# Output projection of a slot-attention and feed-forward kernel: from float32 products to three float32r products on 12-bit parts, added to the residual stream in DRAM

## The chip, the cores and the metric

One core of a Trainium2 chip. The metric is the device time of one launch in microseconds (us); the engines that matter are TensorE (PE in the profile, with its weight loads PEld), VectorE (DVE), ScalarE (ACT), GpSimd (POOL) and SyncE (SP, which only issues DMAs here).

## The reference, cut to what matters

Four samples (b = 0 to 3) of 512 tokens by 512 features. Each goes through an attention block with 16 heads and then a feed-forward block, both behind a layer norm and both added to the residual stream.

```
x = x + attention(layernorm(x))
x = x + ffn(layernorm(x))

attention(x):
  q, k, s = x @ Wq, x @ Wk, clip(x @ Ws, -32, 32)       # per head 64 wide
  v, g    = x @ Wv, x @ Wg                               # per head 128 wide
  o  = softmax(causal (q k^T) over slots weighted by exp(s)) applied to v in the same causal way
  o  = o * rsqrt(mean(o^2) + eps) * g_norm_weight
  o  = o * g * sigmoid(g)
  return o @ Wo                                          # 2048 -> 512
ffn(x): silu(x @ fp8(gate) * gs) * (x @ fp8(up) * us) @ fp8(down) * ds
```

The output projection `o @ Wo` and the gate `g = x @ Wg` are what the change touches. All inputs are float32.

## The kernel before, in words

**Units.** The attention works on units: a unit is a pair of heads (g = 0 to 7, HG = 2 heads) of one sample b. They run in the order of two halves: all eight g for samples 0 and 1 in turn ((0,0), (0,1), (1,0), ... (7,1)), then all eight g for samples 2 and 3. That makes 32 units. In units with an even g the values of two head pairs are projected at once (four `project_v`); units with an odd g have no value projection and are shorter. The feed-forward block of all four samples follows, in 12 chunks of 128 hidden features per sample.

**Precision by parts.** A projection such as q, k, s, g or v does not run in float32. Activation and weight are each kept as a rounded high part, a remainder and a mixed third matrix, all float32r; `Projection.main` (L463) accumulates two products per 128-row chunk into one PSUM bank, `Projection.mixed` (L475) a third product into another, ScalarE scales the first bank out (L473), and VectorE subtracts the second (L483). `project_v` (L504) does the same for v. The weights are split once, in the first half, by pieces of 512 columns in `load_matrix` (L222: one ScalarE and two VectorE operations a piece), written to DRAM, and read back already split in the second half. The small attention products (`states`, `diagonal_blocks`, `slot_scores`, `read_out`) and the transposes are plain float32.

**The output projection.** `turn_output` (L746) transposes the scaled head output into PSUM and VectorE multiplies it by the norm weight and by the gate `sg` into `oT` (L751). `project_output(n)` (L756) multiplies, for each of four blocks n of 128 tokens, `oT` with `w_o` in float32, one matmul per head (L760), and VectorE adds the PSUM bank to the residual tile `x1[b]` in SBUF (L768). All four samples' residual streams stay in SBUF for the whole kernel. A unit's own output is projected during the next unit (`before` in `attention`).

**Order.** The order of the work is written out by hand in `attention` (L773): every engine runs its instructions in exactly this order. Side work (splitting weights in the first half; in the second half rounding the feed-forward weights to fp8 in `quantize`, L401, six VectorE operations a piece) lies in a list, and `other()` takes the next step of it at fixed places. PSUM has a pool of three banks with the tag `proj` (all projections), three single banks for transposes and small products, and two accumulators.

The tail of a unit in this order, before the change:

```
X.slot_scores(); X.value_states()
X.gate_main(0); X.softmax(); X.gate_mixed(0); X.gate_silu(0); output(...)
X.gate_main(1); X.slot_weights(); X.softmax_sum(); X.gate_mixed(1); X.gate_silu(1); exp_and_log()
output(...); X.weight_slot(); output(3); X.read_out()
```

`slot_scores` (L629) makes the scores (`ps_ok`), VectorE scales them (`okT`, L652); `softmax` (L654) transposes them (`ps_okn`), VectorE takes the maximum (L659) and subtracts it (L661), ScalarE exponentiates (L664); `slot_weights` (L676) transposes back (`ps_w`) and VectorE scales (`wT`, L681); `weight_slot` (L683) makes the masked blocks `b` (L542); `read_out` (L686) the head output (`ps_ov`), whose squares ScalarE takes (L714) for the norm; the `pow` of the norm runs on GpSimd (L719). `gate_silu` switches ScalarE's function table and `exp_and_log` switches it back.

Of the kernel before, what the change touches and what calls it, by code (L numbers as in the profile page):

```python
# [49 lines left out]
def kernel(  # L50
# [37 lines left out]
    resid = ctx.enter_context(tc.tile_pool(name="resid", bufs=1))  # L88
# [48 lines left out]
    dsc = const.tile([P, D], F32, tag="dsc", name="dsc")  # L137
# [6 lines left out]
    def load_scales():  # L144
        nc.gpsimd.dma_start(dsc, down_scale.partition_broadcast(P))
        nc.gpsimd.dma_start(srow[0:NFC, :], gate_scale.rearrange("(c p) -> c p", p=P))
        nc.gpsimd.dma_start(srow[NFC : 2 * NFC, :], up_scale.rearrange("(c p) -> c p", p=P))
        nc.gpsimd.dma_start(srow[2 * NFC : NS, :], g_norm.rearrange("(c p) -> c p", p=P))
# [12 lines left out]
    MATRICES = {"s": (Ws, HM), "k": (Wk, HM), "q": (Wq, HM), "v": (Wv, 2 * HV), "g": (Wg, HV)}  # L161
    wt = {}
    split = {}
    wo = {}
# [17 lines left out]
    for g in range(NG):  # L182
        names = [nm for nm in MATRICES if nm != "v" or g % 2 == 1]
        if g == 0:
            names = "v"
        for nm in names:
            n = g if nm != "v" else 0 if g == 0 else (g + 1) // 2
            if nm != "v" or n < NG // 2:
                parts = max(1, KC * MATRICES[nm][1] // RAW)
                to_fetch += [(nm, n, part, KC // parts) for part in range(parts)]  # L190
    fetched = [0]

    def fetch():
        if to_fetch:
            nm, g, part, chunks = to_fetch.pop(0)
            src, width = MATRICES[nm]
            tag = f"raw{fetched[0] % 2}"
            fetched[0] += 1
            w = one.tile([P, RAW], F32, tag=tag, name=f"raw_{nm}_{g}_{part}")[:, : chunks * width]
            rows = src[part * chunks * P : (part + 1) * chunks * P, g * width : (g + 1) * width]  # L200
            nc.sync.dma_start(
                w.rearrange("p (c n) -> p c n", c=chunks), rows.rearrange("(c p) n -> p c n", p=P)
            )
            raw.setdefault((nm, g), []).append(w)

    def fetch_first():

        for tag, names in (("og", "sk"), ("oT", "q"), ("sg", "g")):
            w = one.tile([P, 2, RAW // 2], F32, tag=tag, name=f"raw_{names}")
            for i, nm in enumerate(names):  # L210
                src, width = MATRICES[nm]
                to = w[:, i, :] if nm != "g" else w.rearrange("p i n -> p (i n)")
                nc.sync.dma_start(
                    to.rearrange("p (c n) -> p c n", c=KC),
                    src[:, :width].rearrange("(c p) n -> p c n", p=P),
                )
                raw[nm, 0] = [to]
            if names == "q":
                fetch()
                fetch()  # L220

    def load_matrix(nm, g, first):  # L222
        width = MATRICES[nm][1]
        w = one.tile([P, 3, KC * width], F32R, tag=f"w_{nm}", name=f"w_{nm}_{g}")
# [5 lines left out]
        pieces = KC * width // 512  # L230
# [9 lines left out]
        def rest(n):  # L240
            cols = slice(n * 512, (n + 1) * 512)
            hi, lo = w[:, 0, cols].bitcast(F32), w[:, 1, cols].bitcast(F32)
            if scale == 1.0:
                nc.vector.tensor_tensor(w[:, 1, cols], source(n), hi, ALU.subtract)
            else:
                nc.vector.scalar_tensor_tensor(
                    w[:, 1, cols], source(n), scale, hi, ALU.mult, ALU.subtract
                )
            nc.vector.scalar_tensor_tensor(w[:, 2, cols], hi, DELTA, lo, ALU.mult, ALU.subtract)
            if (n + 1) * 512 % RAW == 0 or n + 1 == pieces:  # L250
                if g > 0 or nm == "v":
                    fetch()
            if n + 1 == pieces:
                split[nm, g] = dram.tile(
                    [P, 3, KC * width], F32, tag=f"split_{nm}_{g}", name=f"split_{nm}_{g}"
                )
                nc.sync.dma_start(split[nm, g], w.bitcast(F32))
# [10 lines left out]
    def load_wo(g):  # L268
        wo[g] = one.tile([P, HG, D], F32, tag="w_o", name=f"w_o_{g}")
        nc.sync.dma_start(wo[g], Wo[g * HV : (g + 1) * HV, :].rearrange("(c p) n -> p c n", p=P))  # L270

# [9 lines left out]
    x1 = [resid.tile([P, NT, D], F32, tag=f"x1_{b}", name=f"x1_{b}") for b in range(B)]  # L281
# [104 lines left out]
    staged = []  # L386

    def stage():
        if to_round:
            c, m = to_round.pop(0)  # L390
            cols = slice(c * P, (c + 1) * P)
            tag = "qw" if (3 * c + m) % 2 else "raw0"
            w = one.tile([P, D], F32, tag=tag, name=f"qw_{c}_{m}")
            if m < 2:
                src = (gate_w, up_w)[m][:, cols].rearrange("(c p) n -> p c n", p=P)
                nc.sync.dma_start(w.rearrange("p (c n) -> p c n", n=P), src)
            else:
                nc.sync.dma_start(w, down_w[cols, :])
            staged.append((c, m, w))
# [169 lines left out]
    class Heads:  # L569


        def __init__(self, g, b):
            self.u, self.g, self.b = f"{g}_{b}", g, b
            self.v0 = g % 2 * HV

# [158 lines left out]
        def gate_main(self, h):  # L734
            if h == 0:
                self.sg = one.tile([P, HG, T], F32, tag="sg", name=f"sg_{self.u}")
            self.pg = Projection("g", self.b, h * DV, f"g_{self.u}_{h}")
            self.pg.main(self.sg[:, h, :])
# [4 lines left out]
        def gate_silu(self, h):  # L743
            nc.scalar.activation(self.sg[:, h, :], self.sg[:, h, :], AF.Silu)

        def turn_output(self, h, n_bank=None):  # L746

            if h == 0:
                self.oT = one.tile([P, HG, T], F32, tag="oT", name=f"oT_{self.u}")
            pt = transpose_4(self.og[:, h], f"ps_oT_{self.u}_{h}", n_bank)  # L750
            nc.vector.scalar_tensor_tensor(  # L751
                self.oT[:, h, :], pt.rearrange("p n t -> p (n t)"), gw, self.sg[:, h, :],
                ALU.mult, ALU.mult,
            )

        def project_output(self, n):  # L756

            pp = ps3.tile([P, D], F32, tag="proj", name=f"ps_o_{self.u}_{n}")
            for h in range(HG):
                nc.tensor.matmul(  # L760
                    pp,
                    self.oT[:, h, n * P : (n + 1) * P],
                    wo[self.g][:, h, :],
                    start=(h == 0),
                    stop=(h == HG - 1),
                )
            to = x1[self.b][:, n, :]
            nc.vector.tensor_tensor(to, to, pp, ALU.add)  # L768
# [4 lines left out]
    def attention(g, b, before, load):  # L773
# [5 lines left out]
        def output(n):  # L779
            if before:  # L780
                before.project_output(n)

# [20 lines left out]
        X.queries(None)  # L803
        load("q")
        X.turn_e()
        if even:
# [10 lines left out]
            if before:  # L817
                before.turn_output(1)
            X.query_key()
            X.values(2)  # L820
            other()
            next_step()
            X.values(3)
            load("v")
            if b > 1:
                other(1)
        else:
            if before:
                before.turn_output(0)
            X.turn_k()  # L830
            if before:
                before.turn_output(1)
            X.key_states()
            X.inverse()
            X.query_key()
            output(0)
            other()
            next_step()
            output(1)
        other()  # L840
        X.slot_scores()
        next_step()
        X.value_states()
        other()
        next_step()
        need("g")
        X.gate_main(0)
        X.softmax()
        X.gate_mixed(0)
        other()  # L850
        X.gate_silu(0)
        output(0 if even else 2)
        if before:
            next_step()
        X.gate_main(1)
        X.slot_weights()
        X.softmax_sum()
        X.gate_mixed(1)
        load("g")
        X.gate_silu(1)  # L860
        exp_and_log()
        if even:
            output(1)
            other()
            output(2)
        X.weight_slot()
        output(3)
# [23 lines left out]
    def ffn_hidden(b, c):  # L891
# [12 lines left out]
        tag = ("sg", "og", "oT")[at] if at >= 0 else ("raw0", "raw1")[c % 2]  # L904
# [6 lines left out]
    def ffn_down(b, chunks, sums):  # L911
# [37 lines left out]
    with tc.manual_schedule(engines=EVERY):  # L949
        blocks = x[0].rearrange("(n p) d -> p n d", p=P)  # L950
        for n in range(NT):
# [3 lines left out]
        load_wo(0)  # L955
        layernorm(0, 1)
        for nm in "vgskq":
            load_matrix(nm, 0, True)
        for b in range(1, B):
            nc.sync.dma_start(x1[b], x[b].rearrange("(n p) d -> p n d", p=P))  # L960
# [5 lines left out]
        for i, (g, b) in enumerate(units):  # L966
            last = i + 1 == len(units)

            def load(nm):
# [5 lines left out]
                elif nm == "o":  # L975
                    if b % 2 == 0 and i > 0:
                        load_wo(g)
# [3 lines left out]

            if i == 0 or (g, b) == (0, 2):
# [19 lines left out]
            if i == 0:  # L1002
                scale_columns()
        while work:
# [10 lines left out]
        for b in range(B):  # L1015
            need(f"xs_{b}")
            for c in range(NFC):
# [3 lines left out]
                if b == 0 and 0 < c < 3:  # L1021
                    before.turn_output(c - 1, 2)
                if b == 0 and 2 < c < 3 + NT:
                    before.project_output(c - 3)
                if c == 1 and b + 1 < B:
                    layernorm(b + 1, 2, 2)()
                if prev is not None:
# [8 lines left out]
                    else:  # L1036
                        ffn_down(pb, [(pc, parts)], sums)
# [3 lines left out]
        ffn_down(B - 1, kept + [(c, h)], sums)  # L1041
# [43 lines left out]
```

## Time and profile before

| | |
|---|---|
| median of 3 runs | 1526.57 us (1526.57 to 1530.5) |
| the profiled execution | 1527.82 us |
| its span in the trace | 1526.1 us |
| granted TensorE clock, mean | 0.996 |
| GpSimd busy | 78.5 us, 77 instructions |
| DMA moved | 149.51 MB, mean 98 GB/s |
| first score product of a split unit / first feed-forward product | 61.2 us / 1242.2 us |
| a unit with even g, second half (786.21 to 829.27 us) | 43.06 us |
| a unit with odd g, second half (721.63 to 753.92 us) | 32.29 us |

How to read the profile's lines: a group of instructions is given as line, engine, operation, output<-inputs by the program's names, shapes and count; then busy time and mean duration of one in ns; then the engine's idle time just before them and what ended it. In a timeline each row is a start, a duration, and the same description. A float32 matmul of 128x512 leaves two records, a float32r one leaves one; durations of matmuls overlap (the next starts before the end of the last), so the distance from one group's start to the next group's start is what a group costs TensorE.

### The profile page before, as it was taken

How to read it: one execution, taken by the hardware profiler on the slowest of the kernel's cores; microseconds unless marked ns; L12 is line 12 of the kernel's file. 1: busy time of each engine (PE TensorE's matmuls, PEld its weight loads, DVE VectorE, ACT ScalarE, POOL GpSimd, SP SyncE). 2: the span in 40 equal slices, each digit the busy share in tenths (PEclk: the TensorE clock that was granted, in tenths of full speed). 3: DMA queues.
4: the chain of work that ended last, by engine and by line, in shares of the span. 5: the costliest groups of instructions: out<-in, count | busy, mean ns of one | idle time of the engine just before them, and what ended most of it. 6: DMA issues, size and time to landing. Idle time of an engine off the chain costs nothing.

```text
span 1526.1 us, 21595 instructions
## 1 busy us (share of the span) xinstructions
PE 1495.5 (98%) x8821; PEld 1131.9 (74%) x8821; DVE 1014.9 (66%) x1814; ACT 558.2 (37%) x942; POOL 78.5 (5%) x77
## 2 busy tenths in 40 slices
PE   7899999999999999999999999999999999999998
PEld 4677777777777777777777777777777777888886
DVE  7677747774777477676877787778777754535333
ACT  4534333433443343442433243333333332222321
POOL 1000000000000000000000000000000000000000
PEclk9999999999999999999999999999999999999999
DMA  8133303330333052115232522243234220000000
GB/s 330 63 111 152 138 15 111 152 138 14 111 152 139 15 207 77 49 42 207 68 120 84 199 81 106 104 179 100 87 116 153 77 104 1 28 0 28 1 28 28
DMA packets 59842, 149.51 MB, mean 98 GB/s; under 512 B 3848, under 2 KB 32544, under 8 KB 56672
## 3 DMA queue, kind: packets, MB, share of 16 engines
q1 hardware_dynamic: 59280, 147.34, 26.5%
q8 instruction: 69, 1.13, 0.3%
q10 hardware_dynamic: 288, 0.52, 0.1%
q0 software_dynamic: 176, 0.28, 0.1%
q14 instruction: 29, 0.24, 0.0%
HBM read 90.45 MB, written 57.67 MB: 97 GB/s over the span
## 4 chain that ended last, share of the span: by engine, by line
PE 91%; DVE 5%; ACT 3%; issue 1%; DMA 0%; POOL 0%; ACTq 0%; DVEq 0%; POOLq 0%
PE ps_o L760 15%; PE ps_v L511 8%; PE ps_g L468 8%; PE ps_fu L880 5%; PE ps_fg L880 5%; PE ps_ov L704 4%; PE ps_v_m L511 4%; PE ps_g_m L479 4%; PE ps_s L468 3%; PE ps_k L468 3%; PE ps_q L468 3%; PE ps_fd L924 2%; PE ps_a L538 2%; PE ps_fe L924 2%; PE ps_b L538 2%; PE ps_ok L644 2%
## 5 line engine op out<-in xcount | busy, mean ns | idle before, releaser
L760 PE MATMUL ps_o<-w_o,oT 128*128 128x512 f32 x512 | 242.0, 604 | 0.0
L760 PEld LDWEIGHTS ps_o<-w_o,oT 128*128 128x128 f32 x512 | 93.2, 189 | 85.6 <-issue 75.5
L468 PE MATMUL ps_g<-xs,w_g 128*128 128x512 f32 x512 | 144.4, 423 | 0.3
L511 PE MATMUL ps_v<-w_v,xs 128*128 128x512 f32 x512 | 132.9, 401 | 0.0
L768 DVE TENSOR_TENSOR x<-x,ps_o 128x512 f32<-128x512 f32 x128 | 87.7, 685 | 56.9 <-PE ps_o L760 56.8
L468 PEld LDWEIGHTS ps_g<-xs,w_g 128*128 128x128 f32 x512 | 93.3, 188 | 36.5 <-issue 18.2
L473 ACT ACTIVATE sg<-ps_g 128x512 f32<-128x512 f32 x64 | 38.2, 597 | 214.0 <-PE ps_g L468 213.1
L719 POOL TENSOR_TENSOR rs<-rs,mhalf 128x8 f32<-128x8 f32 x32 | 56.0, 1750 | 1095.1 <-DVE rs L716 920.3
L901 DVE SCALAR_TENSOR_TENSOR h<-ps_fu,scol,act 128x512 f32<-128x512 f32 x48 | 36.0, 750 | 113.8 <-PE ps_fu L880 111.2
L511 PEld LDWEIGHTS ps_v<-w_v,xs 128*128 128x128 f32 x512 | 92.3, 188 | 20.3
L520 DVE TENSOR_TENSOR v<-v,ps_v_m 128x512 f32<-128x512 f32 x64 | 44.0, 688 | 94.5 <-PE ps_v_m L511 94.5
L519 ACT ACTIVATE v<-ps_v 128x512 f32<-128x512 f32 x64 | 38.4, 600 | 163.6 <-PE ps_v L511 163.6
L880 PE MATMUL ps_fg<-xs,wf 128*128 128x512 f32 x384 | 96.5, 393 | 0.0
L880 PE MATMUL ps_fu<-xs,wf 128*128 128x512 f32 x384 | 95.1, 390 | 1.1 <-ACT act L898 1.1
L880 PEld LDWEIGHTS ps_fu<-xs,wf 128*128 128x128 f32 x384 | 72.0, 188 | 16.7 <-ACT act L898 1.5
L880 PEld LDWEIGHTS ps_fg<-xs,wf 128*128 128x128 f32 x384 | 71.1, 188 | 14.5
L714 ACT ACTIVATE og<-ps_ov 128x512 f32<-128x512 f32 x64 | 38.2, 598 | 118.4 <-PE ps_ov L704 118.4
L715 DVE TENSOR_REDUCE rs<-og 128x4 f32<-128x512 f32 x64 | 43.9, 686 | 54.8 <-ACT og L714 54.8
L479 PE MATMUL ps_g_m<-xs,w_g 128*128 128x512 f32 x256 | 75.3, 416 | 0.0
L704 PE MATMUL ps_ov<-v,b 128*128 128x128 f32 x512 | 67.3, 286 | 3.0 <-DVE b L542 3.0
L511 PE MATMUL ps_v_m<-w_v,xs 128*128 128x512 f32 x256 | 68.8, 391 | 0.0
L468 PE MATMUL ps_s<-xs,w_s 128*128 128x512 f32 x248 | 65.8, 407 | 2.4 <-ACT xs L343 2.4
(149 smaller groups left out, 2759.2 us busy)
## 6 DMA issues: line engine op xcount, KB each, us to landing
split_v<-w_v SPq DMA_DIRECT2D x4, 3072.0 KB, 10.9
split_g<-w_g SPq DMA_DIRECT2D x8, 1536.0 KB, 6.1
w_v<-split_v SPq DMA_DIRECT2D x4, 3072.0 KB, 10.7
w_g<-split_g SPq DMA_DIRECT2D x8, 1536.0 KB, 6.7
rounded<-qw SPq DMA_DIRECT2D x36, 256.0 KB, 2.0
wf<-rounded SPq DMA_DIRECT2D x12, 768.0 KB, 5.9
w_o<-in_L_attn_Wo_dram SPq DMA_DIRECT2D x16, 512.0 KB, 3.6
split_s<-w_s SPq DMA_DIRECT2D x8, 768.0 KB, 4.2
```

The source lines that it names most:

```text
L468: nc.tensor.matmul(self.p, products(self.nm, c, self.col0, i), xs[self.b][i][:, c, :], start=(i == 0 and c == 0), stop=(i == 1 and c == KC ...
L479: nc.tensor.matmul(self.m, products(self.nm, c, self.col0, 2), xs[self.b][2][:, c, :], start=(c == 0), stop=(c == KC - 1),)
L511: nc.tensor.matmul(dst, xs[b][i][:, c, n * P : (n + 1) * P], wt["v"][:, i, c * 2 * HV : (c + 1) * 2 * HV], start=(i == which[0] and c == 0 ...
L520: nc.vector.tensor_tensor(to, to, m, ALU.subtract)
L538: nc.tensor.matmul(pa[h][:, n, :], lT[rows, cols], rT[rows, cols], start=True, stop=True)
L704: nc.tensor.matmul(po[h][:, n, :], self.bb[h][:, n, :], both_v[self.b][:, n, self.v0 + h * DV : self.v0 + (h + 1) * DV], start=False, stop ...
L715: nc.vector.tensor_reduce(rs[:, h, :], self.og[:, h], AX.X, ALU.add)
L719: nc.gpsimd.tensor_tensor(rs, rs, mhalf.rearrange("p (h n) -> p h n", h=HG), ALU.pow)
L760: nc.tensor.matmul(pp, self.oT[:, h, n * P : (n + 1) * P], wo[self.g][:, h, :], start=(h == 0), stop=(h == HG - 1),)
L768: nc.vector.tensor_tensor(to, to, pp, ALU.add)
L880: nc.tensor.matmul(pp, w[:, c * P : (c + 1) * P], xs[b][k][:, c, :], start=(c == 0 and k == 0), stop=(c == KC - 1 and k == 1),)
L924: nc.tensor.matmul(sums[n], parts[k][:, n * P : (n + 1) * P], fw[c][2], start=(c == 0 and k == 0), stop=(c == NFC - 1 and k == 1),)
```

## The change

- `Wo` becomes a sixth matrix of `MATRICES`, split by `load_matrix` like the others (two pieces of 512 columns for each g, written to DRAM in the first half and read back in the second, 1.5 MB instead of 0.5 MB).
- `turn_output` now writes gate times output into `sg` in place; `high_output` and `split_output` make the three parts of `oT` from it: per head two ScalarE and two VectorE operations more.
- `project_output(n)` does six float32r matmuls into two `proj` banks (four into `p`, two into `m`) instead of two float32 ones into one; ScalarE scales `p` into an SBUF tile `y` (two buffers).
- `add_output(n)` (new) subtracts `m` from `y` on VectorE, and a GpSimd DMA with `accum_op=add` adds `y` to `stream[b]`, a copy of the sample's residual stream in DRAM (filled by DMA from `x`). The four resident tiles are gone: `load_tokens` reads a sample's stream into one of two `x1` buffers when a layer norm needs it.
- In `attention` both gate halves and their silu move ahead of `slot_scores`; all four `output(n)` now stand between `softmax` and `read_out`, in even and odd units alike. Places of `other()` move too: one now lies behind the q projection, and in even units one lies behind `value_states`.

```diff
-    MATRICES = {"s": (Ws, HM), "k": (Wk, HM), "q": (Wq, HM), "v": (Wv, 2 * HV), "g": (Wg, HV)}
+    MATRICES = {"s": (Ws, HM), "k": (Wk, HM), "q": (Wq, HM), "g": (Wg, HV), "v": (Wv, 2 * HV), "o": (Wo, D)}
+    CHUNKS = {nm: HG if nm == "o" else KC for nm in MATRICES}
...
-    x1 = [resid.tile([P, NT, D], F32, tag=f"x1_{b}", name=f"x1_{b}") for b in range(B)]
+    stream = [dram.tile([T, D], F32, tag=f"stream_{b}", name=f"stream_{b}") for b in range(B)]
+    x1 = {}
+    def load_tokens(b, source):
+        x1[b] = two.tile([P, NT, D], F32, tag="x1", name=f"x1_{b}")
+        nc.sync.dma_start(x1[b], source[b].rearrange("(n p) d -> p n d", p=P))
...
             nc.vector.scalar_tensor_tensor(
-                self.oT[:, h, :], pt.rearrange("p n t -> p (n t)"), gw, self.sg[:, h, :],
+                self.sg[h], pt.rearrange("p n t -> p (n t)"), gw, self.sg[h],
                 ALU.mult, ALU.mult,
             )
+        def high_output(self, h):
+            nc.scalar.mul(self.oT[:, 0, h, :], self.sg[h], UNDER)
+        def split_output(self, h):
+            hi, lo, less = (self.oT[:, i, h, :] for i in range(3))
+            nc.vector.tensor_tensor(lo, self.sg[h], hi.bitcast(F32), ALU.subtract)
+            nc.vector.scalar_tensor_tensor(
+                less, lo.bitcast(F32), -1.0 / DELTA, hi.bitcast(F32), ALU.mult, ALU.add
+            )
+            nc.scalar.mul(lo, lo.bitcast(F32), 1.0 / DELTA)
         def project_output(self, n):
-            pp = ps3.tile([P, D], F32, tag="proj", name=f"ps_o_{self.u}_{n}")
-            for h in range(HG):
-                nc.tensor.matmul(pp, self.oT[:, h, n * P : (n + 1) * P], wo[self.g][:, h, :], ...)
-            to = x1[self.b][:, n, :]
-            nc.vector.tensor_tensor(to, to, pp, ALU.add)
+            p = ps3.tile([P, D], F32, tag="proj", name=name)
+            m = ps3.tile([P, D], F32, tag="proj", name=name + "_m")
+            for dst, which in ((p, (0, 1)), (m, (2,))):
+                for i in which:
+                    for h in range(HG):
+                        nc.tensor.matmul(dst, self.oT[:, i, h, n * P : (n + 1) * P],
+                            wt["o"][:, i, h * D : (h + 1) * D], ...)
+            y = two.tile([P, D], F32, tag="y", name=f"y_{self.u}_{n}")
+            nc.scalar.mul(y, p, 1.0 + DELTA)
+            self.y[n] = y, m
+        def add_output(self, n):
+            y, m = self.y.pop(n)
+            nc.vector.tensor_tensor(y, y, m, ALU.subtract)
+            nc.gpsimd.dma_start(stream[self.b][n * P : (n + 1) * P, :], y, accum_op=ALU.add)
```

The new order in `attention`, from the key states on, for a unit with odd g (even units have the same tail; their parts of `oT` are made between the value projections):

```diff
+            before.high_output(0)
+            before.high_output(1)
+            X.query_key()
+            before.split_output(0)
+            before.split_output(1)
             X.inverse()
...
+        X.gate_main(0); X.gate_mixed(0); X.gate_main(1); X.gate_mixed(1)
+        X.gate_silu(0); X.gate_silu(1); exp_and_log()
         X.slot_scores()
         X.value_states()
+        if even: other()
         X.softmax()
+        output(0)
+        before.project_output(1)
         X.slot_weights()
+        before.add_output(1)
         X.softmax_sum()
+        output(2)
         X.weight_slot()
         other()
+        output(3)
         X.read_out()
```

## The prediction, before the changed kernel had run

> **What bounds the kernel now.** I read the page's busy shares and the chain that ended last, then the PE timeline of one unit, then the DVE and ACT timelines of the same unit, and last the list of DMA issues.
>
> ```profile
> PE 1495.5 (98%) x8821; PEld 1131.9 (74%) x8821; DVE 1014.9 (66%) x1814; ACT 558.2 (37%) x942; POOL 78.5 (5%) x77
> ...
> PE 91%; DVE 5%; ACT 3%; issue 1%; DMA 0%; POOL 0%; ACTq 0%; DVEq 0%; POOLq 0%
> ```
>
> TensorE is the bound, and by the chain it waits for almost nobody. VectorE has a third of the span free, but not evenly: in the second half it is busy 25.70 us of an odd unit's 32.29. The PE timeline of that odd unit (start, duration):
>
> ```profile
> 724.45 1.98 PE L468 MATMUL ps_k<-xs,w_k 128*128 128x512 f32 x8
> 726.26 1.07 PE L479 MATMUL ps_k_m<-xs,w_k 128*128 128x512 f32 x4
> 727.17 1.98 PE L468 MATMUL ps_q<-xs,w_q 128*128 128x512 f32 x8
> ...
> 733.75 3.70 PE L760 MATMUL ps_o<-w_o,oT 128*128 128x512 f32 x8
> 737.38 0.87 PE L637 MATMUL ps_ok<-qT,sk 64*64 64x128 f32 x12
> 738.18 1.09 PE L644 MATMUL ps_ok<-a,e 128*64 128x128 f32 x16
> 739.11 0.82 PE L552 MATMUL ps_sv<-v,e 128*64 128x128 f32 x12
> 739.86 2.13 PE L468 MATMUL ps_g<-xs,w_g 128*128 128x512 f32 x8
> 741.83 0.60 PE L528 MATMUL ps_okn<-ident,okT 128*128 128x128 f32 x4
> ...
> 743.21 1.88 PE L760 MATMUL ps_o<-w_o,oT 128*128 128x512 f32 x4
> 744.52 2.42 PE L468 MATMUL ps_g<-xs,w_g 128*128 128x512 f32 x8
> 746.77 0.60 PE L528 MATMUL ps_w<-ident,ok 128*128 128x128 f32 x4
> ```
>
> Every group starts where the last one's stream ends: TensorE is never short of work, because gate products and output blocks lie between the links of the softmax chain. Costs follow from start to start. Twelve float32r products of k take 727.17 - 724.45 = 2.72 us, 0.227 each. Two float32 output blocks take 737.38 - 733.75 = 3.63, 1.82 a block.
>
> **TensorE's gain.** A block becomes six float32r products: 6 x 0.227 = 1.36. Going from float32 to float32r and back costs extra: g's first eight products, after `ps_sv`, take 1.97 where k's take 1.81, and a mixed group ahead of float32 1.02 instead of 0.91; call it 0.15 in, 0.10 out. The four output blocks stand in three runs, so 4 x 1.36 + 3 x 0.25 = 6.19, against 3.63 + 1.31 + 1.91 = 6.85 now (the last block 749.33 to 751.24). The gate, now in one run, falls from 1.97 + 1.02 + 2.25 + 1.11 = 6.35 to 5.70. Gain 1.3 in an odd unit; the same sum in an even one gives 1.4. I take **1.35 a unit, 43 us in 32 units**.
>
> **What the new order uncovers.** The gate no longer stands between the scores and their transpose.
>
> ```profile
> 739.39 0.69 DVE L652 TENSOR_TENSOR okT<-ps_ok,rzT 128x512 f32<-128x512 f32 x1 [0.15 <-PE ps_ok L644]
> ...
> 742.47 0.69 DVE L659 TENSOR_REDUCE mx<-ps_okn 128x8 f32<-128x512 f32 x1 [0.21 <-PE ps_okn L528]
> 743.19 0.69 DVE L661 TENSOR_TENSOR ok<-ps_okn,mx 128x512 f32<-128x512 f32 x1
> ```
> ```profile
> 743.92 0.63 ACT L664 ACTIVATE ok<-ok 128x512 f32<-128x512 f32 x1 [1.29 <-DVE ok L661]
> ```
>
> (A) Put the new order on these times. `okT` ends at 740.08, while `ps_sv` ends at 739.86: `ps_okn` waits 0.27 to 740.13. VectorE has the sums of `sv` until 740.94 (its rows L563 and L565), then maximum and subtraction to 742.36, ScalarE the exponential to 743.03, and behind it on ScalarE's queue stands the scaling of the first block's `p` (0.60, as L473) to 743.65. TensorE does `ps_okn` to 740.49, block 0 to 742.0, block 1's `p` to 742.9, and then block 1's `m`: of three `proj` banks it gets the one that block 0's `p` held, so it waits for that scaling until 743.7, 0.8 us. Queued behind `m` is `ps_w`, and so the rest of the unit. A costs 1.07 a unit.
>
> (B) Odd units only. ScalarE's second halves of the two `lo` parts stand ahead of gate 0's scaling-out, and gate 1's mixed product needs that bank. From the end of the `ps_a` products (733.75): hand-over 0.2, two masks 1.3, four VectorE split operations at 0.66 = 2.6, `lo` 0.6, gate 0 0.6: 739.1. TensorE gets there at 733.75 + 1.97 + 0.91 + 1.81 = 738.4. B costs 0.75. In even units the splits lie between value projections, with 0.4 to spare by the same sum: nothing; if that cover were gone, 0.6.
>
> (C) Side work moves into the chain. Second half, even units: two rounding operations (L424, L425: 1.3) between `sv` and the maximum, lengthening A: 7 x 1.3. Odd units: L412 and L413 (0.7) ahead of the q subtraction, which leaves about 0.35 late: 7 x 0.35. First half: a weight piece on ScalarE (0.6) between exponential and scaling in some five odd units: 3. Together 15.
>
> (D) The added DMAs. Nothing like an accumulating DMA is in this trace. `y` has two buffers, so ScalarE's scaling of block 2 waits until block 0's DMA has landed; block 3's `m` waits for the bank which that scaling frees, and on VectorE the masks of `b` stand behind block 2's subtraction. Count from the end of block 0's scaling: subtraction 0.69, then L (hand-over to GpSimd and landing), scaling 0.6 and two hand-overs of 0.05: `m` can start at 1.39 + L. TensorE meanwhile does `m` 0.55, `ps_w` 0.36, block 2's 1.6, `ps_b` 1.1 and block 3's `p` 1.06, arriving at 4.7. **The wait is L - 3.3 in each of 31 units.** Next by size:
>
> ```profile
> raw_sk<-in_L_attn_Ws_dram SPq DMA_DIRECT2D x1, 256.0 KB, 5.1
> ...
> dsc<-in_L_ffn_down_scale_dram POOLq DMA_DIRECT2D x1, 256.0 KB, 6.1
> ```
>
> Upper end: GpSimd's one 256 KB DMA took 6.1, but in the start-up traffic, when SP's loads of that size took 5.1 too (3.1 later: `raw_s`); plus 0.17 hand-over, L = 6.3. Lower end: the Trainium skill, "DMA: Bandwidth & Descriptors", section "Anatomy of one DMA — SWDGE (gpsimd) path", gives a GpSimd DMA 2.0 us plus its bytes at 436 GB/s: 2.6, an estimate from that page, so L = 2.8 and no wait at all. By the rule D costs 0, by the row 31 x 3.0 = 93. Value: a 256 KB store by SP takes 2.0 (`rounded`), GpSimd's path about 0.8 more (6.1 against 5.1 to 5.5), reading the destination first 1.1 more (a load's 3.1 against a store's 2.0), hand-over 0.17, and 0.35 for weight loads beside it (`w_o` triples): L = 4.4, nearer the row when its start-up share is taken off. D costs 31 x 1.1 = 34. A second rule speaks against the change: "SBUF — State Buffer", section "Who interferes with whom", says that VectorE operations in its two-port mode keep GpSimd from writing descriptors. No row here shows it; the candidates are the 0.42 us rounding operations, so it can add some tenths in the second half, inside my upper end.
>
> GpSimd's `pow` (1.67) queues behind block 3's DMA issue (0.76 for `dsc`), yet VectorE uses its result 0.9 us after it ends today: hidden, at worst 0.7 a unit. The other additions are hidden too: VectorE's block subtractions replace the additions one for one (685 ns each), ScalarE's 8 x 0.6 us a unit meet an engine busy 12.4 of 32.3 us, except where A and B name them.
>
> (E) Edges. Splitting the first `w_o` adds four VectorE operations (2.8) at the start, where VectorE is busy 38 of 50 us. In the feed-forward part the stream loads for samples 2 and 3 wait on the SP queue for the stores of an earlier sample, and VectorE's queue holds their statistics ahead of the hidden products: about 2 each. The last unit's projection there: about 1. Together 8; from 0 to 15.
>
> **The sum.** Odd: 16 x (-1.35 + 1.07 + 0.75) = +7.5. Even: 15 x (-1.35 + 1.07) = -4.2. C +15, D +34, E +8: +60. On the profiled execution's 1527.8 (span 1526.1 and 1.7 around it) 1588; the median was 1.2 lower: **1586**.
>
> **Rivals.** (1) *L below 3.3.* D vanishes, A to C and E stay: 1526.6 + 26 = 1553. For it: the rule above; against it: 6.1 in the trace. (2) *Faster: TensorE stays the bound.* One place decides, block 1's `m`: if block 0's scaling is done when TensorE arrives, so that A (0.8) goes and every later anchor of D moves 0.8 forward with L under 2.5, odd units gain 0.3 and even ones 1.1, and with TensorE filling the rest of the gaps the whole 43 less E is gained, 1526.6 - 35 = 1492. The tipping point is waits of 1.35 a unit. For it: L760 and the projections show no idle time today, and ScalarE is 37% busy. Against: the chain, whose links are all measured, is longer than the 3.5 us of work left beside it. (3) *The accumulating DMA is as slow as at start-up*, 6.3: 1526.6 + 26 + 93 = 1645.
>
> **Numbers.** The likeliest case, L from 3.3 to 5.5, 1553 to 1620: 0.55. Rival 1, 1532 to 1553: 0.15. Rival 2, 1480 to 1522: 0.15. Rival 3 and beyond, over 1620: 0.10. Gain and waits cancelling, within 0.3% (about what a measurement of this kernel can tell from no change): 0.05. So faster 0.15, same 0.05, slower 0.80. The range 1512 to 1645 leaves out most of rival 2 and the tail of rival 3.
>
> **What would show it.** Right: block products at 0.227 us each and no `ps_o` group over 1.6; TensorE idle before `ps_okn` (0.3) and before the second `ps_o` m-group (0.8) released by ScalarE; in odd units idle before gate 1's mixed product; ScalarE's third `y` released by a GpSimd DMA, with L - 3.3 of TensorE idle before the fourth m-group; odd units of 33 to 35 us. Wrong: even units of 41.7 us without idle time (rival 2), or a landing time under 3 or above 6 us.

## The result, and the profile after

The changed kernel takes **1681.93 us** (median; 1680.6 to 1690.7) against 1526.99 (1526.57 to 1530.5) for the kernel before: ratio **1.102**, 95% interval 1.098 to 1.106. The profiled execution has a span of 1680.0 us (before 1526.1, so +153.9) and a mean granted clock of 0.969 (before 0.996). I had forecast 1586, and at most 1645. Slower was right; the size was not.

The page of the changed kernel, busy times and the chain that ended last (line numbers are those of the changed kernel):

```profile
PE 1505.5 (90%) x9077; PEld 1196.7 (71%) x9077; DVE 1112.8 (66%) x1974; ACT 701.3 (42%) x1214; POOL 191.4 (11%) x204
...
issue 44%; PE 28%; DVE 11%; DMA 10%; POOL 3%; ACT 3%; POOLq 0%; ACTq 0%; DVEq 0%; SPq 0%
```

TensorE no longer owns the chain (91% before, 28% now), and it is busy longer although its work became shorter: the larger part of that is the clock, as shown below. Its idle time went from 30.6 to 174.5 us. Where it sits is in the costliest groups (busy, mean ns of one | idle time before them and what ended it):

```profile
L796 POOL DMA_DIRECT2D stream<-y x128 | 110.9, 867 | 1110.9 <-DVE y L795 1109.3
L795 DVE TENSOR_TENSOR y<-y,ps_o_m 128x512 f32<-128x512 f32 x128 | 87.4, 683 | 147.7 <-ACT y L790 139.7
L782 PE MATMUL ps_o_m<-w_o,oT 128*128 128x512 f32 x256 | 90.8, 437 | 91.2 <-ACT y L790 91.1
L790 ACT ACTIVATE y<-ps_o 128x512 f32<-128x512 f32 x128 | 72.4, 590 | 210.2 <-DMA stream<-y 201.9
```

Read from the bottom: ScalarE's scaling of a block into `y` waits 201.9 us in all for an accumulating DMA, and TensorE's mixed products of output blocks wait 91.1 us for that scaling. No other group of TensorE waits more than 15.1 us. A block is one of the four output blocks of 128 tokens, numbered 0 to 3. Taking the 91.1 apart by block in the PE timeline gives 26.4 us before block 1 (31 times, steps A and C of the prediction) and 64.8 before block 3 (step D): **20.8 in 21 units, up to 1.3 each, and 44.0 in only seven units**, 4.9 to 7.6 each. I number the units 0 to 31 in the order of work; the seven are 6, 10, 13, 17, 21, 25, 29, and the others are called quiet below. Here is 17, its PE timeline:

```profile
796.37 0.73 PE L782 MATMUL ps_o_m<-w_o,oT 128*128 128x512 f32 x2 [1.76 <-ACT y L790]
...
799.96 1.19 PE L782 MATMUL ps_o<-w_o,oT 128*128 128x512 f32 x4
807.49 1.22 PE L782 MATMUL ps_o_m<-w_o,oT 128*128 128x512 f32 x2 [6.34 <-ACT y L790]
808.64 1.65 PE L703 MATMUL ps_ov<-sv,wT 64*128 64x128 f32 x12
810.22 3.37 PE L712 MATMUL ps_ov<-v,b 128*128 128x128 f32 x16
```

and what stands behind it, in the timelines of ScalarE, GpSimd and SP:

```profile
806.84 0.60 ACT L790 ACTIVATE y<-ps_o 128x512 f32<-128x512 f32 x1 [10.03 <-DMA stream<-y]
```
```profile
797.34 0.89 POOL L796 DMA_DIRECT2D stream<-y  x1 [33.27 <-DVE y L795]
```
```profile
789.08 0.32 SPq L228 DMA_DIRECT2D w_g<-split_g  x1
789.45 0.42 SPq L228 DMA_DIRECT2D w_v<-split_v  x1
```

Block 0's DMA is issued at 797.34 and has landed at 806.8, after 9.4 us. Eight microseconds earlier SP had issued 1.5 MB of `w_g` and 3 MB of `w_v`. The stretches of that unit (length, busy time and count of PE, PEld, DVE, ACT, POOL, then clock, DMA share, GB/s) show the transfer, the standstill and its consequence:

```profile
798.00:802.00 4.00, 3.15 (x25) 2.06 (x23) 1.63 (x4) 0.00 (x0) 1.08 (x2) 1.00 1.04 344
802.00:806.00 4.00, 0.00 (x0) 0.00 (x0) 0.00 (x0) 0.00 (x0) 0.00 (x0) 1.00 0.94 205
806.00:813.00 7.00, 5.51 (x27) 4.64 (x28) 2.52 (x5) 1.79 (x3) 1.70 (x2) 0.51 0.68 107
```

From 798 to 806 the DMA engines are taken almost throughout (share 1.04 and 0.94), and from 802 to 806 no compute engine does anything. Then the clock is halved, from 806.2 to 813.0; this begins while TensorE still stands, as the single microseconds show:

```profile
805.00:806.00 1.00, 0.00 (x0) 0.00 (x0) 0.00 (x0) 0.00 (x0) 0.00 (x0) 1.00 1.10 219
806.00:807.00 1.00, 0.00 (x0) 0.00 (x0) 0.00 (x0) 0.16 (x1) 0.00 (x0) 0.59 0.44 82
807.00:808.00 1.00, 0.51 (x1) 0.50 (x2) 0.53 (x1) 0.43 (x1) 0.00 (x0) 0.50 0.05 8
```

TensorE then works 5.5 us at half clock: the `ps_ov` group of 1.65 + 3.37 us takes 0.94 + 2.05 at full clock. Units 6 and 10 have the 3 MB store of `split_v` beside their blocks, 13, 17, 21 and 25 a reload of `w_v`, and 29 a reload of `w_g` with 3 MB of rounded feed-forward weights behind it. Over the span 107.8 us pass at half clock, against 13.1 before. TensorE's products ran in 76.2 of them (9.9 before), in the rest it stood still. So the work lost at half clock, half of that running time, is about 38.1 us against 4.9: +33. The losses at half clock given below are counted in this way.

### The profile page after: what moved, and what is told of

It reads as the page before. It is cut to its first block, busy times and chain, and to the rows that moved or that the text cites. A ratio compares the mean times of both kernels' runs of the same rounds, so it can differ in the third digit from the quotient of the medians.

```text
span 1680.0 us, 23077 instructions
## 1 busy us (share of the span) xinstructions
PE 1505.5 (90%) x9077; PEld 1196.7 (71%) x9077; DVE 1112.8 (66%) x1974; ACT 701.3 (42%) x1214; POOL 191.4 (11%) x204
## 4 chain that ended last, share of the span: by engine, by line
issue 44%; PE 28%; DVE 11%; DMA 10%; POOL 3%; ACT 3%; POOLq 0%; ACTq 0%; DVEq 0%; SPq 0%
DMA stream<-y 9%; PE ps_fg L920 4%; PE ps_fu L920 4%; POOL rs L727 3%; PE ps_v L517 2%; PE ps_ov L712 2%; PE ps_fe L964 2%; PE ps_fd L964 2%; DVE rs L723 2%; DVE y L795 1%; ACT y L790 1%; DVE b L548 1%; PE ps_ov L703 1%; PE ps_v_m L517 1%; PE ps_g L474 1%
## 5 line engine op out<-in xcount | busy, mean ns | idle before, releaser
L796 POOL DMA_DIRECT2D stream<-y x128 | 110.9, 867 | 1110.9 <-DVE y L795 1109.3
L795 DVE TENSOR_TENSOR y<-y,ps_o_m 128x512 f32<-128x512 f32 x128 | 87.4, 683 | 147.7 <-ACT y L790 139.7
L782 PE MATMUL ps_o_m<-w_o,oT 128*128 128x512 f32 x256 | 90.8, 437 | 91.2 <-ACT y L790 91.1
L790 ACT ACTIVATE y<-ps_o 128x512 f32<-128x512 f32 x128 | 72.4, 590 | 210.2 <-DMA stream<-y 201.9
L782 PE MATMUL ps_o<-w_o,oT 128*128 128x512 f32 x512 | 150.3, 415 | 0.1
L782 PEld LDWEIGHTS ps_o_m<-w_o,oT 128*128 128x128 f32 x256 | 45.7, 198 | 123.2 <-ACT y L790 116.5
L474 PE MATMUL ps_g<-xs,w_g 128*128 128x512 f32 x512 | 131.1, 399 | 0.0
L517 PEld LDWEIGHTS ps_v<-w_v,xs 128*128 128x128 f32 x512 | 92.3, 188 | 20.4
L772 ACT ACTIVATE oT<-oT 128x512 fp32r<-128x512 f32 x64 | 40.5, 633 | 132.8 <-DVE oT L769 132.8
L947 ACT CAST both<-h 128x512 fp32r<-128x512 f32 x48 | 29.8, 621 | 109.7 <-DVE h L941 109.7
L489 DVE TENSOR_TENSOR sg<-sg,ps_g_m 128x512 f32<-128x512 f32 x64 | 43.9, 685 | 43.6 <-PE ps_g_m L485 41.4
## 6 DMA issues: line engine op xcount, KB each, us to landing
split_v<-w_v SPq DMA_DIRECT2D x4, 3072.0 KB, 10.6
```

Of the source, the lines that this page charges most:

```text
L474: nc.tensor.matmul(self.p, products(self.nm, c, self.col0, i), xs[self.b][i][:, c, :], start=(i == 0 and c == 0), stop=(i == 1 and c == KC ...
L489: nc.vector.tensor_tensor(self.to, self.to, self.m, ALU.subtract)
L517: nc.tensor.matmul(dst, xs[b][i][:, c, n * P : (n + 1) * P], wt["v"][:, i, c * 2 * HV : (c + 1) * 2 * HV], start=(i == which[0] and c == 0 ...
L782: nc.tensor.matmul(dst, self.oT[:, i, h, n * P : (n + 1) * P], wt["o"][:, i, h * D : (h + 1) * D], start=(i == which[0] and h == 0), stop= ...
L790: nc.scalar.mul(y, p, 1.0 + DELTA)
L795: nc.vector.tensor_tensor(y, y, m, ALU.subtract)
```

## The experiments

**Theory 1**: `y`, with two buffers, is held until the accumulating DMA has landed; these waits and the half clock behind the long ones are most of the loss. **Theory 2**: the moved gate leaves the softmax's chain uncovered. **Theory 3**: the long landings come from weight transfers beside the DMA, not from the adding. Times are medians; before took 1527.8 to 1528.0 in these series. Differences between two changed kernels are between their medians; the runs of one such kernel lie up to 14 us apart, so a few us between two of them are not settled.

**Four buffers for y.**

```diff
-            y = two.tile([P, D], F32, tag="y", ...)
+            own = n < 2 or (self.g, self.b) == (NG - 1, B - 1)
+            y = (two if own else one).tile([P, D], F32, tag="y" if own else "kT" if n == 2 else "qT", ...)
```

> Blocks 2 and 3 get buffers of their own for y (the tiles of kT and qT, idle at that time); nothing else changes. Theory 1 (the two buffers of y, held until the accumulating DMA has landed, carry most of the loss): the waits before the fourth block's mixed products go, 0.8 to 1.2 us in about 24 units and 4.9 to 7.6 in seven, together about 70, and with them most of the half-clock stretches behind them, about 30 more: 1682 - 100 = about 1582, clock above 0.985. Theory 2 (the softmax chain, shortened of its cover by moving the gate): no more than 10 us faster, and the same idle time appears elsewhere in the unit.

Measured **1593.76** (ratio to before 1.043, 1.039 to 1.046), clock 0.985. What TensorE waits for at these products is now block 1 alone:

```profile
PE ps_o_m L782 <- ACT y L793: 26.4, 31, 1.8
```

The 64.8 us before block 3 are gone to the last one, and the loss at half clock fell from 38.1 to 17.6: 85 by this count, 91.5 less span, 88 less time. Theory 1 holds, and theory 2 isn't the main part.

**Writing without adding.**

```diff
-            nc.gpsimd.dma_start(stream[...], y, accum_op=ALU.add)
+            nc.gpsimd.dma_start(stream[...], y)
```

> GpSimd's DMAs write y without adding; the residual addition of the attention is left out of the computation. If the reading of the destination is what makes the transfer long, the landing falls from 4.3 to about 3.2 us, the quiet waits of about 1 us go (24 us) and the loaded ones shrink by 1 us: about 1650. If it is the software queue and the traffic beside it, the landing stays above 4 us and the time within 10 us of 1682.

This kernel leaves out the residual addition of the attention. Measured **1637.34**, 45 less. The DMA's row in the changed kernel, and here:

```profile
stream<-y POOLq DMA_DIRECT2D x128, 256.0 KB, 4.3
...
stream<-y POOLq DMA_DIRECT2D x128, 256.0 KB, 2.3
```

The landing fell from 4.3 to 2.3 us, more than I expected, and the quiet waits before block 3 from 20.8 to 0.7. The seven long ones stayed, 38.6 for 44.0. So adding costs 2.0 us a DMA, which explains the quiet waits; the long ones do not come from adding. These waits are 25 of the 45 us; the rest was not taken apart.

**Weight reloads later in the program.**

```diff
-        load("g")
-        if even:
-            load("v")
+        late = b > 1 or g >= NG - 2
+        if not late:
+            load("g")
+            if even:
+                load("v")
...
         X.read_out()
+        if late:
+            load("g")
+            if even:
+                load("v")
```

> The reloads of w_g and w_v in the second half (and at the end of the first) are issued at the end of the unit, behind all four accumulating DMAs, instead of just ahead of the first one; y keeps two buffers. Theory 3 (those transfers beside block 0's DMA make its landing 8 to 11 us): units 13, 17, 21, 25 and 29 fall from 50 to 54 us to about 45, their share of the half-clock stretches goes: 1682 - 40 = about 1640. Units 6 and 10, where a store of split_v collides, stay at 43.6. If the long landings come from something else (VectorE beside GpSimd, say): within 10 us of 1682, with long landings in the same units.

Measured **1701.58**, 20 more than the changed kernel: as a remedy a failure. Yet units 21 and 25 fell from 52.3 and 53.7 us to 45.2 and 45.1, as theory 3 says. The landing of block 0's DMA in unit 21, in the changed kernel and here:

```profile
DMA to landing us min/median/max: 8.7/8.7/8.7
...
DMA to landing us min/median/max: 4.1/4.1/4.1
```

In 25 it falls from 9.7 to 4.0 and in 29 from 7.9 to 4.9, where the loads did move; in 13, where they are still issued at 600.3, 7 us ahead of that DMA, it stays at 8.0. But units 22 and 26 rose from 33.4 and 33.8 to 46.9. In 22, SP's queue and VectorE:

```profile
979.59 0.42 SPq L228 DMA_DIRECT2D w_v<-split_v  x1
982.52 0.38 SPq L402 DMA_DIRECT2D qw<-in_L_ffn_gate_w_dram  x1
```
```profile
998.61 0.43 DVE L418 TENSOR_SCALAR q<-qw 128x512 int32<-128x512 int32 x1 [11.28 <-DMA qw<-in_L_ffn_gate_w_dram]
```

The collision moved to another victim: a 256 KB piece for the rounding lands 16 us after its issue, and VectorE's queue, with the output's split in it, stands behind that. Unit 17 didn't improve either (landing 13.6, and its block 3 waited 10.57): a later place in the program isn't a later time on SP, which issued the loads at 796.4, among the output blocks, right behind the store that is ahead of them in its queue. Theory 3 holds for the cause: in five units the long landing stays or goes with the transfers. That the units add up to a gain was wrong.

**The gate back between the softmax's steps**, with four `y`: `gate_main(0)` ahead of `softmax`, gate 1 around `slot_weights`, each SiLU after its subtraction.

> As the kernel with four y, and the gate's products put back between the softmax's steps, as before. Theory 2 (the moved gate uncovers the chain): against the kernel with four y the waits before the transposed scores (0.27), before block 1's mixed products (0.43 to 1.76) and before gate 1's mixed product (0.3 to 0.45) go, less 0.5 us a unit for more changes between float32r and float32: 15 to 25 us faster, about 1560. Theory 1 (with y out of the way little is left): within 10 us of the kernel with four y.

Measured **1666.78**, 73 more than with four `y`. The 26.4 us before block 1 are gone, so the moved gate did uncover them; but 38.4 us before block 2's mixed products and 13.1 before `ps_okn` stand in their place:

```profile
PE ps_o_m L782 <- ACT y L793: 38.4, 28, 1.4
PE ps_okn L534 <- DVE okT L660: 13.1, 14, 1.0
```

Theory 2's remedy falls, though this run also has `kT` waiting for `y`'s DMA (4.4 us in unit 26), so it is repeated below in a kernel without that.

**The border of the halves**: with four `y`, and

```diff
+            if (g, b) == (0, 2):
+                need("xs_2")
```

> As the kernel with four y (1594), and the last operations of sample 2's layer norm are put on VectorE's queue ahead of sample 3's statistics, at the start of unit 16. Theory (the wait of 8.1 us at the start of unit 16 comes from that order, sample 3's statistics standing ahead of the last split of sample 2): the wait falls to about 1 us, unit 16 from 60.6 to about 52 and the half-clock stretch of 10.2 us behind it goes (5 us): 1594 - 12 = about 1582. If the statistics are simply late for want of places for side work, the wait stays above 5 us and the time within 4 us of 1594.

Measured **1589.63**, 4 less, which is within the scatter (ratio 1.040, 1.039 to 1.042). Unit 16 did fall, from 60.6 to 54.9, and its first wait from 8.1 to 2.7; the span, 1588.5 and 1589.2, did not. The order was part of that unit's wait; a gain in the whole isn't shown.

**Scaling ahead of the exponential** (step A), with four `y`: `softmax` is cut before its exponential, and

```diff
-        output(0)
         if before:
+            before.project_output(0)
+        X.softmax_exp()
+        if before:
+            before.add_output(0)
             before.project_output(1)
```

> As the kernel with four y, and ScalarE's scaling of output block 0 is put ahead of the softmax's exponential on its queue. Step A of the prediction (block 1's mixed products wait for the bank that this scaling frees): the wait before them, 0.4 us in quiet units and 1.5 to 1.8 in the even units of the second half, goes in 31 units: 15 to 20 us faster, about 1576. Rival: the exponential, later by 0.3, makes the transposed weights wait in its place: no faster than 1590.

Measured **1571.76**, 22 less. The waits before block 1 fell from 26.4 to 1.7 us; those before the transposed weights rose from 2.5 to 8.2, so the rival was there too, at a quarter of the size:

```profile
PE ps_w L534 <- ACT ok L674: 8.2, 9, 2.5
PE ps_o_m L784 <- ACT y L795: 1.7, 1, 1.7
```

**Side work off the chain** (step C), with four `y`:

```diff
-        X.queries(None if before is None else other)
+        X.queries(other if before and even else None)
...
-        if even:
-            other()
         next_step()
         X.softmax()
-        if not even:
-            other()
+        other()
```

(and one `other()` ahead of the scores in odd units).

> As the kernel with four y, and the side work is moved off the chain: in even units from between the slot values' sums and the maximum to behind the exponential's input, in odd units from the query projection to behind the gate. Step C of the prediction: seven even units of the second half 1.0 to 1.3 each, the three odd units 3, 7 and 11 about 2 each, other odd units 0.35: about 15 us faster, 1579. If side work only takes free time of VectorE: within 4 us of 1594.

Measured **1573.93**, 20 less (the spans 1588.5 and 1574.8). The wait before block 1 fell by 7.4 us in all, and the waits before `ps_sk`, in units such as 3, 7 and 11, from 9.0 to 4.1:

```profile
PE ps_o_m L782 <- ACT y L793: 19.0, 31, 1.7
PE ps_sk L558 <- DVE sg L758: 4.1, 12, 0.3
```

**The three together**, and gate 0's scaling ahead of the low parts' (step B).

> As the kernel with four y, with the three changes together (border, scaling ahead of the exponential, side work moved) and, in odd units, ScalarE's scaling of the two low parts put behind gate 0's scaling-out (step B, 0.35 in 16 units): if the parts add up, 12 + 17 + 15 + 5 = about 49 us faster than 1594, 1545. If A and C are the same wait counted twice: about 1555. Even units of the second half then take 42 us against 43.06 before the change.

Measured **1530.53** (ratio 1.0019, 1.0008 to 1.0029): 63 less than with four `y`, more than the 49 of my sum. Even units of the second half take 41.8 us.

**Other tiles for y.** In the kernel with the three together, `kT` still waits 14.1 us and `qT` 5.4 for `y`'s DMAs; so `"ok"` and `"e"` in place of `"kT"` and `"qT"`.

> The kernel with all changes so far (1530.5), with y of blocks 2 and 3 in the tiles of the softmax's ok and of e in place of kT and qT: those are written again some 20 and 9 us into the next unit, not 5 and 8. If what is left of theory 1 is the next unit's kT and qT waiting for those DMAs to land (14.1 and 5.4 us in the waits of the run before, and a half-clock stretch or two), 15 to 20 us faster: about 1513. If the release of y no longer matters: within 4 us of 1530.

Measured **1522.30** (ratio 0.9966, 0.9955 to 0.9976): 8 less, half of what I expected, and below the kernel before.

**Four edges** on top of that.

```diff
+        if work and work[0][0].startswith("xs_"):
+            other(1)
         X.read_out()
...
-                if b == 0 and 2 < c < 3 + NT:
-                    before.project_output(c - 3)
+                if b == 0 and 3 < c < 4 + NT:
+                    before.project_output(c - 4)
...
```

(and: statistics of the next sample at c == 4, three chunks behind their load; gate 1 behind the softmax in unit 0).

> The kernel just named, and four edges: the last split of a new sample's layer norm issued at the end of the unit before; in unit 0, which has no output blocks to cover the softmax, gate 1 put back behind the softmax; in the feed-forward part the last unit's blocks one chunk later and the next sample's statistics three chunks behind its load. Step E of the prediction (edges): unit 0 from 53.8 to about 50, units 1 and 16 each 2 us less, feed-forward part 5 to 8 less, 14 us together: about 1500, faster than the kernel before the change (1527.8). If the edges hold nothing that can be had: within 4 us of the kernel just named.

Measured **1503.93** (ratio **0.985**, 0.984 to 0.986): 18 less, clock 0.996, loss at half clock 4.5. This is the fastest version, 1.5% faster than the kernel before the change. Its output blocks in odd unit 18, PE timeline:

```profile
733.28 1.17 PE L787 MATMUL ps_o<-w_o,oT 128*128 128x512 f32 x4
734.29 0.62 PE L787 MATMUL ps_o_m<-w_o,oT 128*128 128x512 f32 x2
734.74 1.07 PE L787 MATMUL ps_o<-w_o,oT 128*128 128x512 f32 x4
735.65 0.62 PE L787 MATMUL ps_o_m<-w_o,oT 128*128 128x512 f32 x2
```

From start to start block 0 takes 1.46 and no group waits: this is the order that the changed kernel lacked.

**The fastest version with y in two buffers again**, which is step D by itself.

> The kernel with all changes and edges (1503.9), with y back in two buffers: step D by itself, the rest of the unit being free of other waits. If D is an independent term (quiet wait about 1.0 in some 24 units, 4.9 to 7.6 in seven units beside weight transfers, half-clock stretches behind those, about 20 to 30): 70 to 100 slower, about 1590. If the other waits had hidden or caused part of it: under 50 slower, below 1554.

Measured **1621.34**, **117 more**.

```profile
PE ps_o_m L787 <- ACT y L795: 84.1, 30, 8.8
```

All of these waits stand before block 3 (62.3 us of them in ten waits over 2 us), and the loss at half clock is 40.2 for 4.5: together 120. Where nothing else makes TensorE late, the two buffers cost more, not less.

**The fastest version with gate 1 back** between block 1 and `slot_weights`, which is theory 2 by itself.

> The kernel with all changes and edges (1503.9), with gate 1's products back between output block 1 and the transposed weights, both SiLUs and the table loads behind its subtraction, as in the kernel before the change. Theory 2 (the moved gate is a cause of the loss): 5 us or more faster. Rival: with the output blocks scaled by ScalarE the two table loads (1.28 each) and SiLUs (0.63 each) now stand ahead of block 2's scaling, 3.8 us against about 2 us of cover, and the gate's place ahead is the right one: 40 to 70 us slower. If the 73 us of the earlier kernel with the gate put back came from kT waiting for y only: within 10 us of 1504.

Measured **1603.31**, **99 more**. TensorE's two largest waits, and ScalarE in unit 22:

```profile
PE ps_okn L534 <- DVE okT L660: 25.9, 19, 2.4
PE ps_o_m L787 <- ACT y L798: 24.4, 30, 0.8
```

```profile
949.38 1.28 ACT L753 ACT_TABLE_LOAD   x1
950.68 0.63 ACT L753 ACTIVATE sg<-sg 128x512 f32<-128x512 f32 x1
951.86 0.63 ACT L753 ACTIVATE sg<-sg 128x512 f32<-128x512 f32 x1 [0.55 <-DVE sg L489]
952.51 1.28 ACT L807 ACT_TABLE_LOAD   x1
953.80 1.09 ACT L798 ACTIVATE y<-ps_o 128x512 f32<-128x512 f32 x2
```

Two table loads and two SiLUs, 4.4 us from start to block 2's scaling, stand ahead of it; block 3's mixed products wait up to 0.8, 24.4 us in 30 units. The same order also delays the scores (25.9 us before `ps_okn`) and puts the loads among the blocks again (17.4 us of waits for `e`, held by `y`, where the fastest version has 6.3), with 20.4 more lost at half clock. So not all 99 are the gate's own; but putting the gate back gains nothing in either kernel. Its place ahead of the scores did uncover block 1's wait, which another order on ScalarE's queue removed (step A); on balance it was no cause of the loss, and the fastest version rests on it.

## Why the prediction was wrong, point by point

- **TensorE's gain: right.** 1.35 us a unit forecast. With nothing else waiting, an even unit falls from 43.06 to 41.84 and an odd one from 32.28 to 31.09: 1.2 each, 38 of the 43 us, with the small waits of the new order in it.
- **A: the mechanism right, the size too large.** I had 1.07 a unit: 0.27 before `ps_okn`, where the quiet units show 0.14, and 0.8 before block 1's mixed products. The whole wait there is 26.4 us, of which 7.4 went with the side work: 19.0, or 0.6 a unit. Taking it away gave 22 us.
- **B: 0.75 in each odd unit forecast (the sum given for it comes to 0.7), 4.4 us measured in all** (13 waits of at most 0.4 before a gate's mixed products), not 12.
- **C: right for the even units** (7.4 measured for 9.1). Its experiment gained in other places too: by unit lengths 8 us in the seven even units, 5 in unit 15, 4 in unit 31, 3 in unit 1 and 3 in units 3, 7 and 11 together, of which 3 in all were in my sum for the first half; unit 16 and some odd units of the second half lost 1 to 3.
- **D: right in the quiet, and it failed as a mean.** "The wait is L - 3.3 in each of 31 units", with L = 4.4, gave 34. In the quiet, landing 4.3 plus the hand-over gives 1.2, and the trace has up to 1.3, 20.8 us in 21 units. But I had put 0.35 us on L "for weight loads beside it", a share for every unit; the runs have no such share, they have seven units in which block 0's DMA lands after 7.9 to 10.6, and 44.0 us of waits in them. The prediction's own sign of being wrong, a landing above 6, does not show in the median of 4.3; it shows in 34 of the 128 DMAs. The order told me so: `load("g")` and `load("v")` stand a few instructions ahead of the first output block after the change. I counted what the DMA costs, not what else is on the engines at that moment, although I had noted that SP's 256 KB loads take 5.1 in the start-up traffic and 3.1 later.
- **The two prices of L.** The Trainium skill, "DMA: Bandwidth & Descriptors", section "Anatomy of one DMA — SWDGE (gpsimd) path", gave an estimate of 2.6 for a GpSimd DMA of this size; the plain write measured 2.3. The rule is good for a write, and no price for the adding came from it. That my L of 4.4 fits the quiet units is partly luck: I had put 2.8 for the plain DMA, which was 2.3, and 1.1 for reading the destination, where adding cost 2.0. The row of 6.1 in start-up traffic was the better guide to the busy units. The prediction's second rule, VectorE keeping GpSimd from its descriptors, was not tried by itself. The trace doesn't speak for it: in the seven units GpSimd is held 0.89 us for block 0's issue, as in the others, VectorE does nothing from 802 to 806 in unit 17, and the long landings follow the transfers.
- **The clock: missing.** The sum has no term for it. About 33 us more than before are lost at half clock, 17 of them in the stretches behind the seven long waits.
- **E: 8 forecast, about 41 measured**: unit 0 +3.8, unit 1 +2.6, unit 15 +5.0, unit 16 +16.0, last unit and feed-forward part +13.7, some of it at half clock. The sample border (units 15 and 16) was not in my list at all. The order of the layer norm's operations is part of it, as the border's experiment shows; that odd units have three of these moved places for side work where they had four may be another part, which was not tried.

The step that failed is D's L: one number, 4.4, for a duration that has two values, 4.3 in the quiet and 7.9 to 10.6 beside the transfers, with the clock, which the sum had at nothing, behind the larger one. D stood in the sum with 34 us, and four buffers gave back 88. The second miss is E, 41 for 8. Of the +154 us, block 3's waits and the half clock together are 98.

## What to carry to other kernels

A buffer that waits for a DMA should be counted at the landing time in the worst traffic that the order puts beside it, not at the mean: ask which large transfers are issued in the 10 us before it, and give the buffer enough copies, in tiles that stand idle, to outlast them. Moving the large transfer is not the same remedy, since the collision finds the next small one in the queue. Add the half clock to the price of a long TensorE wait: here each wait of 4.9 to 7.6 us brought a stretch of 6.8 or 10.2. And an order that is right while VectorE takes results out can be wrong once ScalarE, with its table loads, does.

## What the runs showed of the hardware that I had not expected

- An accumulating DMA of 256 KB by GpSimd lands after 4.3 us (median), a plain one after 2.3; GpSimd is held 867 and 555 ns for the issue.
- Beside 3 to 4.5 MB of weight transfers, block 0's DMA of the same size landed after 7.9 to 10.6 us adding, and after 7.2 to 9.7 without adding; with the loads moved away, after 4.0 to 4.9 (three units).
- Half clock came in stretches of 3.4, 6.8, 10.2 or, twice, 13.7 us, apart from the one that each kernel's end cuts off. Behind the seven waits of 4.9 to 7.6 us it began 2.4 to 5.0 us after TensorE fell idle, while TensorE still stood, and outlasted the wait: 44.0 us of waiting brought about 17 us of lost work.
- The two buffers cost 117 us in the fastest version, where the changed kernel, full of other waits, had said 88. Putting gate 1 back cost 99 there, where putting both gates back had cost 73 in the kernel with four `y`. In these two cases the cost measured in a kernel full of waits was too small for the kernel without them.
